# Memory matrix of the first attention: loaded as 32x32 squares and turned by VectorE instead of turned by TensorE

## The chip, the core and the metric

The kernel runs on one core of a Trainium2 chip. The metric is the device time of one execution in microseconds (us). TensorE (PE in the profile) multiplies matrices into PSUM; VectorE (DVE), ScalarE (ACT) and GpSimd (POOL) work on tiles in SBUF and PSUM; SyncE (SP) and GpSimd issue transfers, which sixteen DMA engines carry out. SP's transfers go through one queue, GpSimd's through another.

## The reference

Two transformer layers follow each other on an input of 2 x 512 rows of 512 values. Only the first attention is touched. It doesn't attend to other rows: each row is looked up in a memory `M` of eight 128x128 matrices.

```python
q = (hidden_states @ Wq.T + bq).reshape(b, s, H, D)     # H = 32, D = 128
sig_q = jax.nn.elu(q) + 1.0
q_sel = sig_q[:, :, ::G, :]                             # 8 of 32 heads, G = 4
num = jnp.einsum('bshd,hde->bshe', q_sel, M)
den = jnp.einsum('bshd,hd->bsh', q_sel, z)[..., None] + EPS
out_heads = jnp.repeat(num / den, G, axis=2)
output = out_heads.reshape(b, s, H * D) @ Wo.T
...
x = _layernorm(x + attention_0(x));  x = _layernorm(x + ffn_0(x))
x = _layernorm(x + attention_1(x));  x = _layernorm(x + ffn_1(x))
```

The feed-forward of layer 0 works with ternary weights and truncated 8-bit values, layer 1 has an ordinary softmax attention with one joint weight `Wqkv` (512 x 384) and an unquantized feed-forward. The result is the (2, 512, 512) tensor after the last layernorm, in 32-bit floats.

## The kernel before

Everything is on one core, with rows in tiles of 128 and features in blocks of 128. The kernel is written in program order; a scheduler orders the instructions of TensorE, VectorE, ScalarE and SP, and only GpSimd keeps the order of the program. `tc.issue_after` ties a step behind another. Tiles come from pools: a tile with the same tag as an older one gets its buffer and waits until that one is no longer read.

**Queries (0 to 62 us).** For each of 8 selected heads `h` and both batch rows `b`, the list `items` gives the order. `main_queries` issues 8 matmuls of 128x512 in split precision (a high part and a rest), ScalarE raises the result (`raise_main`, L364), and one item later `cross_queries` adds 4 more matmuls, ScalarE takes ReLU and exponential (L556, L557), and VectorE joins them to `q` (L560). `query_weights` splits the query weights, a part on ScalarE (L343) and two on VectorE (L344, L348).

**Folding the memory.** Since the four heads of a group share what is retrieved, the output weights of a group are summed first: SP loads half of them (`wos`, L429, 512 KB a head), GpSimd adds the other half with an accumulating transfer (L642), and `sum_weights` on VectorE adds the two halves of the tile (L574). `fold(h)` (L577) then multiplies the turned `M[h]` with this sum on TensorE (`pmw`, L579), and ScalarE writes it to `mw` (L581, L582). The last column of `mw` holds `z`, which GpSimd copies (L644); `mw` shares its buffer with `xt_raw`, the turned first input rows. For `fold`, `M` has to lie transposed: `turn_memory` (L562) turns its eight 128x128 blocks on TensorE against the identity into two PSUM banks, and ScalarE copies them back over `m` (L568).

The loop over `items` fixes what is done beside which item: `turn_memory` at `i == 4`, sums at `SUMS = [5, 6, 7, 8, 10, 11, 12, 13]`, folds at `FOLDS = [7, 8, 9, 10, 12, 13]` and two behind the loop.

**Loads.** SP issues, in this order: rows and query weights, `m` (512 KB, L422), wo0 to wo3, the gate/up weights gu0 to gu3 of layer 0 (L245, 512 KB each), `wqkv` (768 KB, L437), three biases and layer 1's output weight (L438 to L441), wo4 to wo7, and the other gate/up weights. wo4 to wo7 reuse the buffers of wo0 to wo3 and wait for their sums. GpSimd issues the eight accumulating transfers. SP's transfers use eight completion counters in turn, as do GpSimd's: a transfer waits until the one eight places before it on its queue's counters has landed.

**After that**, `read` (L584) multiplies queries with `mw` (L593), divides, adds and normalizes; then follow the feed-forward of layer 0, layer 1's attention and its feed-forward. In these stages rows are already turned in another way, which the change takes up: VectorE transposes each 32x32 square of a tile in place (`nc.vector.transpose`, L708), and `move_squares` (L301) then moves the squares to their turned places by transfers of 128-byte pieces, some issued by SP, some by GpSimd (L316).

Of the kernel before, what the change touches and what calls it, by code (L numbers as in the profile page):

```python
# [10 lines left out]
F32 = mybir.dt.float32  # L11
# [8 lines left out]
P = 128  # L20
B, S, HID = 2, 512, 512
NT = S // P
NK = HID // P
NH, G, D = 8, 4, 128
# [5 lines left out]
LAST = HID - 1  # L30
SQ = 32
# [8 lines left out]
def kernel(  # L40
# [19 lines left out]
    nc = tc.nc  # L60
# [3 lines left out]
    const = ctx.enter_context(tc.tile_pool(name="const", bufs=1))  # L64
# [7 lines left out]

    ident = const.tile([P, P], F32, tag="ident", name="ident")
    ones = const.tile([P, P], F32, tag="ones", name="ones")
    wqkv = const.tile([P, NK, 3 * D], F32, tag="wqkv", name="wqkv")
    bv = const.tile([P, D], F32, tag="bv", name="bv")
    wo1 = const.tile([D, HID], F32, tag="wo1", name="wo1")
    bo = const.tile([P, HID], F32, tag="bo", name="bo")
# [3 lines left out]
    def psum(name):  # L82
        return ps.tile([P, 512], F32, tag="mm", name=name)
# [13 lines left out]
    z = const.tile([D, NH], F32, tag="z", name="z")  # L97
# [141 lines left out]
    def up_weights(gu_in, name, chunks=range(len(CHUNKS))):  # L239
        gus = []  # L240
        for c in chunks:
            i, n = CHUNKS[c]
            gu = wffn.tile([P, 2, NK, n], F32, tag=f"gu{c}", name=f"gu{name}_{c}")
            at = 2 * HID * i
            nc.sync.dma_start(  # L245
                gu.rearrange("p a k i -> p (a k i)"),
                gu_in[at : at + 2 * HID * n].rearrange("(p f) -> p f", p=P),
            )
            gus.append(gu)
        return gus  # L250
# [75 lines left out]
    def pair_tile(name, dtype=F32):  # L326
        return wop.tile([P, 2, HID], dtype, tag="wo", name=name)
# [78 lines left out]
    with tc.tile_pool(name="a0w", bufs=1) as a0w, tc.tile_pool(name="a0", bufs=2) as a0:  # L406
# [12 lines left out]
            elif h == 2:  # L419
                load_x(1)  # L420
        m = a0w.tile([D, NH, D], F32, tag="m", name="m")
        nc.sync.dma_start(m, m_in)  # L422

        wos = []
        for h in range(NH):
            if h == 4:
                gus = up_weights(gu0_in, "0", range(EARLY))
            w = pair_tile(f"wo{h}")
            nc.sync.dma_start(w, wo0_in[h, :, : G // 2, :])  # L429
            wos.append(w)  # L430
# [3 lines left out]
        def late_loads():  # L434

            gus.extend(up_weights(gu0_in, "0", range(EARLY, len(CHUNKS))))
            nc.sync.dma_start(wqkv, wqkv_in.rearrange("(k p) f -> p k f", p=P))  # L437
            nc.sync.dma_start(bqk, bqk_in)  # L438
            nc.sync.dma_start(bv, bv_in.to_broadcast([P, D]))
            nc.sync.dma_start(wo1, wo1_in)  # L440
            nc.sync.dma_start(bo, bo_in.to_broadcast([P, HID]))  # L441


        hosts = [
# [22 lines left out]
        odd = single("t", 2, 2) + host(1)  # L467
# [94 lines left out]
        def turn_memory():  # L562

            for i in range(2):
                pt = psum(f"pt_m_{i}")
                for j in range(4):
                    nc.tensor.transpose(pt[:, ts(j, P)], m[:, 4 * i + j, :], ident)
                nc.scalar.copy(m[:, 4 * i : 4 * i + 4, :].rearrange("d h e -> d (h e)"), pt)  # L568

        def sum_weights(eng, h):  # L570

# [66 lines left out]
        qs = [{}, {}]  # L638
        pq = first_queries()
        mw = a0w.tile([D, NH, HID], F32, tag="mw", name="mw")  # L640
        for h in range(NH):
            nc.gpsimd.dma_start(wos[h], wo0_in[h, :, G // 2 :, :], accum_op=ALU.add)  # L642
            if h == 0:
                nc.gpsimd.tensor_copy(mw[:, :, LAST], z)  # L644
        query_weights(1, lows[1], lows[3])
        items = [(0, 1), (0, 2), (0, 3), (1, 1), (1, 2), (1, 3), (1, 0)]
        items += [(b, h) for h in range(NH // 2, NH) for b in range(B)]
# [4 lines left out]
        for i, (b, h) in enumerate(items):  # L652
# [11 lines left out]
                    later_rows(2 * i + k)  # L664
            if i + 2 < len(items) and items[i + 2][1] not in wq3:
                query_weights(items[i + 2][1], [*lows[3], *made] if i == 0 else ())
            if i == 4:
                turn_memory()
            if i in SUMS:
                with tc.issue_after(step.ins):  # L670
# [14 lines left out]
        fold(6)  # L685
        cross_queries(*held)
        fold(7)
        late_loads()
        order = [(b, t) for b in range(B) for t in range(NT)]
        checks += [(c, a) for c in range(EARLY, len(CHUNKS)) for a in range(2)]  # L690

# [923 lines left out]
```

## Time and profile before

| | us |
|---|---|
| median of 3 runs | 456.64 (455.45 to 456.96) |
| profiled execution | 456.56 |
| its span (first to last instruction) | 454.8 |
| TensorE matmul busy | 447.1 (98% of the span) |
| VectorE busy | 316.1 (69%) |
| ScalarE busy | 260.1 (57%) |
| GpSimd busy | 115.7 (25%) |

The profile shows one execution. A timeline line gives the start, the duration, the engine, the line of the program, the operation, output and input tiles, and how many instructions are merged; in brackets stands how long the engine was idle before and what ended this. Lines with SPq are issues of transfers: their duration is that of the issue, not of the transfer. Matmul ends are modelled, and neighbouring matmuls overlap, so starts are what to compare. A 32-bit matmul counts as two instructions. The strings of digits cut the span into 40 slices of 11.4 us; 9 means 90% busy or more. The chain of waits is followed back from the last instruction. The trace also records each DMA piece (packet) with its queue, size and duration, and the time at which each transfer landed.

### The profile page before, as it was taken

How to read it: one execution, taken by the hardware profiler on the slowest of the kernel's cores; microseconds unless marked ns; L12 is line 12 of the kernel's file. 1: busy time of each engine (PE TensorE's matmuls, PEld its weight loads, DVE VectorE, ACT ScalarE, POOL GpSimd, SP SyncE). 2: the span in 40 equal slices, each digit the busy share in tenths (PEclk: the TensorE clock that was granted, in tenths of full speed). 3: DMA queues.
4: the chain of work that ended last, by engine and by line, in shares of the span. 5: the costliest groups of instructions: out<-in, count | busy, mean ns of one | idle time of the engine just before them, and what ended most of it. 6: DMA issues, size and time to landing. Idle time of an engine off the chain costs nothing.

```text
span 454.8 us, 5802 instructions
## 1 busy us (share of the span) xinstructions
PE 447.1 (98%) x1905; PEld 334.6 (74%) x1905; DVE 316.1 (69%) x629; ACT 260.1 (57%) x494; POOL 115.7 (25%) x160
## 2 busy tenths in 40 slices
PE   8999999999999999999999999999999999999995
PEld 8887753344587888888766578888888888888884
DVE  4976657877886798847989899545534447777424
ACT  5788986467466975557745645454645446442311
POOL 0200305566650059201473237000000000012211
PEclk9999999999999999999999999999999999999998
DMA  8999990020028101131593502200000000000101
GB/s 280 386 270 317 180 333 8 0 38 12 1 47 235 42 2 48 48 94 38 176 350 69 94 1 43 51 0 1 0 0 1 0 1 1 0 25 24 46 26 68
DMA packets 33300, 38.18 MB, mean 84 GB/s; under 512 B 20784, under 2 KB 21680, under 8 KB 33264
## 3 DMA queue, kind: packets, MB, share of 16 engines
q1 hardware_dynamic: 30736, 31.05, 20.8%
q0 software_dynamic: 2240, 6.29, 7.5%
q8 instruction: 22, 0.36, 0.4%
q10 hardware_dynamic: 288, 0.36, 0.2%
q14 instruction: 14, 0.11, 0.1%
HBM read 32.45 MB, written 2.10 MB: 76 GB/s over the span
## 4 chain that ended last, share of the span: by engine, by line
PE 89%; ACT 5%; DMA 2%; issue 1%; DVE 1%; SPq 0%; POOL 0%; POOLq 0%
PE pu L1307 24%; PE pd L1307 12%; PE po L593 10%; PE pg_f L787 9%; PE pu_f L787 9%; PE pq L538 6%; PE pd_f L846 4%; PE pqk L1120 3%; ACT tu L374 2%; PE pu L1352 2%; PE pv L1137 2%; PE pot L1182 2%; PE po L1199 2%; PE psc L1076 2%; DMA wq<-in_wq 1%; DMA gu<-in_gu 1%
## 5 line engine op out<-in xcount | busy, mean ns | idle before, releaser
L593 PE MATMUL po<-mw,q 128*128 128x512 f32 x128 | 57.3, 599 | 0.3 <-DVE x L615 0.2
L146 POOL TENSOR_TENSOR rstd_f<-mv_f,ln_eps 128x1 f32<-128x1 f32 x15 | 6.7, 450 | 166.7 <-DVE mv_f L1475 128.7
L1307 PE MATMUL pu<-r,ugu 128*128 128x512 f32 x200 | 48.6, 389 | 0.0
L364 ACT ACTIVATE pu<-pu 128x512 f32<-128x512 f32 x42 | 24.2, 581 | 41.5 <-PE pu L1307 37.7
L593 PEld LDWEIGHTS po<-mw,q 128*128 128x128 f32 x128 | 22.6, 189 | 33.4 <-issue 17.2
L1307 PEld LDWEIGHTS pu<-r,ugu 128*128 128x128 f32 x200 | 37.5, 188 | 7.8
L170 ACT ACTIVATE ta_f<-y_f,below_half 128x512 int8<-128x512 f32 (+1 forms) x22 | 15.9, 722 | 27.4 <-DVE y_f L158 25.1
L615 DVE SCALAR_TENSOR_TENSOR x<-po,den,x 128x511 f32<-128x511 f32 x40 | 29.8, 745 | 1.9
L610 POOL TENSOR_TENSOR y<-y,y 128x511 f32<-128x511 f32 x16 | 21.3, 1333 | 23.9 <-DVE x L615 20.2
L1307 PE MATMUL pu<-r,it_early 128*128 128x512 f32 x104 | 24.9, 389 | 0.0
L1366 DVE TENSOR_TENSOR it_f<-ev,pu 128x512 f32<-128x512 f32 x20 | 13.7, 684 | 15.9 <-PE pu L1307 15.6
L1195 ACT ACTIVATE x<-x,off_f,rstd_f 128x512 f32<-128x512 f32 x7 | 5.7, 816 | 31.6 <-POOL off_f L1194 31.6
L813 DVE SCALAR_TENSOR_TENSOR it_f<-tb_f,ta_f 128x512 fp32r<-128x512 int16 (+1 forms) x22 | 15.6, 708 | 11.7 <-ACT tb_f L171 11.7
L1307 PE MATMUL pd<-ugu,r 128*128 128x512 f32 (+1 forms) x79 | 22.5, 362 | 0.0
L1307 PEld LDWEIGHTS pu<-r,it_early 128*128 128x128 f32 x104 | 19.5, 188 | 4.1
L787 PE MATMUL pg_f<-x,tu 128*128 128x512 f32 x88 | 22.1, 393 | 0.0
L787 PE MATMUL pu_f<-x,tu 128*128 128x512 f32 x88 | 21.7, 389 | 0.0
L376 POOL TENSOR_SCALAR td<-wd,inv_down 128x512 fp32r<-128x512 f32 x11 | 19.9, 1826 | 3.2 <-DVE inv_down L206 3.2
L846 PE MATMUL pd_f<-td,it_f 128*128 128x512 f32 x88 | 20.3, 389 | 0.0
L787 PEld LDWEIGHTS pg_f<-x,tu 128*128 128x128 f32 x88 | 16.4, 188 | 4.0 <-DVE x L615 0.4
L597 ACT ACTIVATE den<-po,den_eps 128x1 f32<-128x1 f32 x64 | 13.9, 272 | 9.3 <-PE po L593 9.1
L787 PEld LDWEIGHTS pu_f<-x,tu 128*128 128x128 f32 x88 | 16.5, 188 | 3.4
(390 smaller groups left out, 1111.2 us busy)
## 6 DMA issues: line engine op xcount, KB each, us to landing
gu<-in_gu SPq DMA_DIRECT2D x20, 512.0 KB, 7.1
wd<-in_wd SPq DMA_DIRECT2D x20, 256.0 KB, 4.9
wo<-in_wo SPq DMA_DIRECT2D x8, 512.0 KB, 8.8
wo<-in_wo POOLq DMA_DIRECT2D x8, 512.0 KB, 9.5
wq<-in_wq SPq DMA_DIRECT2D x8, 256.0 KB, 5.0
x<-in_x SPq DMA_DIRECT2D x7, 256.0 KB, 5.1
out<-x SPq DMA_DIRECT2D x7, 256.0 KB, 2.0
x<-in_bo POOLq DMA_DIRECT2D x4, 256.0 KB, 5.9
```

The lines of the kernel that those rows point to most:

```text
L170: nc.scalar.activation(a[:n], y, AF.Relu, bias=below_half[:n])
L364: return nc.scalar.activation(p, p, AF.Copy, scale=BIG + 1.0)
L376: eng.tensor_scalar(out, w, factor, None, ALU.mult)
L538: done = nc.tensor.matmul(p, w, x, start=(start and i == 0), stop=(i == len(todo) - 1), skip_group_check=not start,)
L593: nc.tensor.matmul(po, qs[b][h0 + j][:, ts(t, P)], mw[:, h0 + j, :], start=True, stop=True,)
L597: nc.scalar.activation(den[:, j : j + 1], po[:, LAST:], AF.Identity, bias=den_eps)
L610: nc.gpsimd.tensor_add(ys[0][:, :LAST], ys[0][:, :LAST], y[:, :LAST])
L615: steps.append(nc.vector.scalar_tensor_tensor(x[:, :LAST], four[j][:, :LAST], d, x[:, :LAST], ALU.mult, ALU.add))
L787: nc.tensor.matmul(pp[a], t[:, a, i % NK, :], x2[b][i], start=(i == 0), stop=(i == 2 * NK - 1),)
L813: nc.vector.scalar_tensor_tensor(it[:n], tb[:n], 128.0, ta[:n], ALU.min, ALU.subtract)
L846: nc.tensor.matmul(pd, inter[b][c][:, ts(t, P)], td[c].bitcast(F32R), start=(c == 0), stop=(c == last),)
L1307: done = nc.tensor.matmul(p, w, x, start=(start and i == 0), stop=(i == n - 1), skip_group_check=not start,)
```

## The change

`M` is no longer loaded as it lies and turned by TensorE. Sixteen transfers load its 32x32 squares to their turned places in a new tile `m_squares`: eight on SP, behind gu0 to gu3, and eight on GpSimd, ahead of the accumulating loads of `wo`. Each moves 8 heads x 32 rows of 128 bytes, 32 KB. VectorE then transposes each square in place with two 128x512 instructions, one for each half of the heads, into `m`. These two stand at `i == 6` instead of `i == 4`; in the built order the first lies on VectorE just ahead of the q and the sum of wo0, the second just behind that sum.

`m_squares` takes the buffer in which `wqkv` was, so `wqkv` is now a tile made in `late_loads`, with the same tag: its load waits for the second transpose and stands between wo4 and wo5 on SP. GpSimd's copy of `z` is moved ahead of everything else in that place.

```diff
-    wqkv = const.tile([P, NK, 3 * D], F32, tag="wqkv", name="wqkv")
+    m_squares = const.tile([P, 3, HID], F32, tag="wqkv", name="m_squares")
...
         m = a0w.tile([D, NH, D], F32, tag="m", name="m")
-        nc.sync.dma_start(m, m_in)
+        def load_memory(eng, odd):
+            dst = m_squares[:, :2].rearrange("p a (h i) -> p (a h) i", i=D)
+            for i in range(P // SQ):
+                for j in range(P // SQ):
+                    if (i + j) % 2 == odd:
+                        eng.dma_start(dst[ts(j, SQ), :, ts(i, SQ)], m_in[ts(i, SQ), :, ts(j, SQ)])
 
         wos = []
         for h in range(NH):
             if h == 4:
                 gus = up_weights(gu0_in, "0", range(EARLY))
+                load_memory(nc.sync, 0)
...
             gus.extend(up_weights(gu0_in, "0", range(EARLY, len(CHUNKS))))
+            wqkv = const.tile([P, NK, 3 * D], F32, tag="wqkv", name="wqkv")
             nc.sync.dma_start(wqkv, wqkv_in.rearrange("(k p) f -> p k f", p=P))
...
+            return wqkv
...
         def turn_memory():
             for i in range(2):
-                pt = psum(f"pt_m_{i}")
-                for j in range(4):
-                    nc.tensor.transpose(pt[:, ts(j, P)], m[:, 4 * i + j, :], ident)
-                nc.scalar.copy(m[:, 4 * i : 4 * i + 4, :].rearrange("d h e -> d (h e)"), pt)
+                turned = m[:, 4 * i : 4 * i + 4, :].rearrange("d h e -> d (h e)")
+                nc.vector.transpose(turned, m_squares[:, i])
...
         mw = a0w.tile([D, NH, HID], F32, tag="mw", name="mw")
+        nc.gpsimd.tensor_copy(mw[:, :, LAST], z)
+        load_memory(nc.gpsimd, 1)
         for h in range(NH):
             nc.gpsimd.dma_start(wos[h], wo0_in[h, :, G // 2 :, :], accum_op=ALU.add)
-            if h == 0:
-                nc.gpsimd.tensor_copy(mw[:, :, LAST], z)
...
-            if i == 4:
+            if i == 6:
                 turn_memory()
...
-        late_loads()
+        wqkv = late_loads()
```

## The prediction

> **What bounds the kernel now.** I read the page first (busy shares, chain), then the chain in order of time around the edited stage, then the timelines of the DMA queues and of VectorE there.
>
> ```profile
> PE   8999999999999999999999999999999999999995
> DMA  8999990020028101131593502200000000000101
> PE 89%; ACT 5%; DMA 2%; issue 1%; DVE 1%; SPq 0%; POOL 0%; POOLq 0%
> ```
>
> TensorE is busy in every fortieth of the span, and 89% of the chain is TensorE: what delays it anywhere is paid in full. The DMA engines are full only in the first six fortieths (to 68 us), and that is where the change works.
>
> ```profile
> 17.75 8.21 PE pq L538 x36
> 25.96 0.87 PE pt_m L567 x8
> 26.83 8.18 PE pq L538 x36
> 35.01 0.86 PE pmw L579 x2
> ```
>
> This is the chain in order of time (start, us). The eight transposes of the memory stand on it with 0.87 us. The first reader of the turned memory is `fold(0)` (pmw, first issued at 34.84 in TensorE's timeline).
>
> ```profile
> 10.47 0.43 SPq L422 DMA_DIRECT2D m<-in_m  x1
> 10.95 2.82 SPq L429 DMA_DIRECT2D wo<-in_wo  x4
> 14.14 2.90 SPq L245 DMA_DIRECT2D gu<-in_gu  x4
> 17.97 0.39 SPq L437 DMA_DIRECT2D wqkv<-in_wqkv  x1
> 19.99 0.34 SPq L438 DMA_DIRECT2D bqk<-in_bqk  x1
> 21.29 1.25 SPq L439 DMA_DIRECT2D bv<-in_bv  x1
> 22.58 3.43 SPq L440 DMA_DIRECT2D wo<-in_wo  x1
> 26.06 3.28 SPq L441 DMA_DIRECT2D bo<-in_bo  x1
> ```
>
> This is SP's queue. It has eight completion counters used in turn, so each transfer is issued only when the eighth before it has landed: wqkv, bqk, bv and wo1 are issued at 17.97, 19.99, 21.29 and 22.58, and the trace's landing records have wo0 to wo3 at 17.96, 19.98, 21.27 and 22.54. The last three issues take 1.25 to 3.43 us instead of 0.33 to 0.5: some 1250 pieces are outstanding then (counting 128 per 128-row load and 512 for wqkv), and the issue finishes as older ones land. The queue is backed up.
>
> ```profile
> L245 SPq DMA_DIRECT2D gu<-in_gu x4: 328/328/328, 14.1 to 16.7; - x4
> DMA to landing us min/median/max: 11.1/15.8/20.0
> ```
>
> The four gate/up loads before it land 11 to 20 us after issue, the last (gu3) at 16.7 + 20.0 = 36.7. In that time (22.6 to 37.8) they share the engines with GpSimd's four accumulating loads of `wo`; by the packet records the slowest engine moves one 4096-byte piece of each in turn (0.16 and 0.33 us), so the 32 pieces per engine of gu0 to gu3 need 14.0 us, 0.44 each.
>
> ```profile
> 29.60 0.69 DVE L348 TENSOR_TENSOR host_x<-host_t,host_t 128x512 fp32r<-128x512 f32 x1 [1.38 <-PE pq L538]
> 30.87 0.69 DVE L560 SCALAR_TENSOR_TENSOR q<-pq,r 128x512 f32<-128x512 f32 x1 [0.58 <-ACT pq L557]
> 31.48 0.68 DVE L574 TENSOR_TENSOR wos<-wo 128x512 f32<-128x512 f32 x1
> ```
>
> This is the place on VectorE where the changed kernel's built order puts the first memory transpose: after the first line, ahead of q and of `sum_weights(0)` (wos), which `fold(0)` reads. The second follows wos. So a late memory blocks not only itself but the sum.
>
> **The change part by part.**
>
> *Taken off.* TensorE: 8 transposes, 0.87 us of the chain. ScalarE: 2 copies of 0.60 us at 27.15, where it idles 0.46 us soon after (before L364 at 28.70): nothing. SP: the 512 KB load of `m`, ahead of wo0 in the queue; by the landing records it took from 15.43 to 16.70, 1.27 us.
>
> *VectorE.* Two 128x512 transposes at 0.71 us (the row of L708). By themselves they cost nothing: idle of 1.38, 0.58 and 0.83 us stands in 28.2 to 33.6, and the rows pushed back (L560, L344) feed TensorE only at 39 us or later. If that cover were gone they would cost 1.4 us.
>
> *GpSimd's queue.* The copy of z (0.55 us) goes first, at about 11.4, when the queries of item 0 release its buffer; then 8 square loads, some 0.7 us each (the row of L316 on POOL, 0.65 to 0.92), to about 18; then the accumulating loads, first issued at 18.27 before. So those start as before. Each square load is one piece of some 2 KB per engine if it is packed like the squares of L316 there (4 KB, about 0.3 us), so eight take some 8 x 0.15 = 1.2 us from the SP queue.
>
> *SP's queue, the step that decides.* The other 8 square loads stand behind gu3, in the place of wqkv. In the built order they wait for the counters of wo0 to wo3 and gu0 to gu3, one each. The eighth can be issued only when gu3 has landed.
> - gu3: if the 1.2 us of GpSimd's squares cancel the 1.27 us of `m`, it lands at 36.7 as before. If the squares cost nothing, the lead of 1.27 us is 8 pieces per engine at the contended 0.44, so 3.5 us: 33.2. Another upper bound is 37.8, when the accumulating loads end. I take 35.5, nearer to 36.7, because GpSimd's squares do have a duration.
> - From there to the last square: an SP square load lands 2.0 us after issue:
>
> ```profile
> xt_f<-squares SPq DMA_DIRECT2D x16, 32.0 KB, 1.9
> ```
>
>  Lower bound 0.1 + 2.0 = 2.1. But each has 256 pieces, twice bqk's, and the queue was full with less: the fifth should finish its issue only when gu3 is through, and sixth to eighth follow at 0.65 each (L316 at 91.9 to 103.2), so 1.35 + 2.0 = 3.35. I take 3.3, by the stretched issues of bv, wo1 and bo in this very place. All 16 loads write both halves, so the first transpose waits for the last: 38.8 (bounds 35.3 and 41.1).
> - Behind it on VectorE: transpose 0.71, q 0.6, wos 0.6 and a signal, 2.0 us in all. `fold(0)` starts at 40.8 (37.3 to 43.1) instead of 34.84: **+6.0 us** (+2.5 to +8.3). This contains the gain of the transposes, which is spent in the wait: TensorE comes to `fold(0)` at 33.97 and idles 6.8 us. After it VectorE's backlog runs at 0.6 each and stays ahead (the sums of `fold(1)` and `fold(2)` end near 43 and 45, needed near 44 and 48).
>
> *TensorE's clock.* It starts slow in this trace and drops again after the last matmul (near 449.1):
>
> ```profile
> 1.05 3.79 PE L113 MATMUL rise<-ones 128*128 128x128 f32 x16 [1.05 <-DVE below_half L108]
> 9.36 2.05 PE L509 MATMUL pq<-xt_raw,wq 128*128 128x128 f32 x16 [0.48 <-ACT xt_raw L484]
> 451.00:453.00 2.00, 0.00 (x0) 0.00 (x0) 0.39 (x1) 0.45 (x1) 0.22 (x1) 0.71 0.24 85
> 453.00:454.80 1.80, 0.00 (x0) 0.00 (x0) 0.00 (x0) 0.00 (x0) 0.00 (x0) 0.50 0.16 51
> ```
>
> Sixteen equal matmuls took 3.79 us at the start and 2.05 later; the seventh number of the windows is the granted clock, 0.50 some 4 us after the end. An idle of 6.8 us should cost one such slow start: 3.79 - 2.05 = **1.7 us** (0 if the clock holds, 1.9 if it lasts a little longer).
>
> *Later parts.* SP waits for the first sum with wo4, for the second transpose with wqkv, and wo5 to wo7 stand behind these: issued from about 40.5 instead of 32.19. The queue is empty then, wo4 lands within 3 us instead of 12.7, its accumulation takes 5.7 (45.48 to 51.19), so its sum is ready near 50, while its turn comes at 48.7 + 6: nothing. If that cover were gone, each us late is a us on `fold(4)`. wqkv is first read at 223.7: nothing. The gate/up loads from chunk 4 on wait for TensorE's last queries and shift with it, as does ScalarE's work on them at 64 to 69, which is on the chain.
>
> **Sum.** The profiled execution took 456.56 us (span 454.8 and 1.76 around it), 0.08 under the median of 456.64. 456.56 + 6.0 + 1.7 = **464.3 us**; by the bounds 459.1 to 466.8.
>
> One rule speaks further against the change. The row: sixteen SP loads of 128-byte pieces landed 1.9 us after issue (median) and the packet records show 13 ns a piece, 16 a load and engine. The Trainium skill's page "DMA: Bandwidth & Descriptors", section Specifications, asks for pieces of at least 512 bytes, since smaller ones are read, changed and written back. If that doubled the last four loads (4 x 0.21 us), the time would be about 465.1; by the row nothing is added. Both sources are in SBUF there, so the trace does not show such pieces read from memory in bulk.
>
> **The rivals.**
> - *The squares arrive in time (faster side).* If GpSimd's squares take turns with the SP queue by their 128-byte pieces, 16 x 8 pieces each behind a 4096-byte one (0.16), they last till after 30, the accumulating loads start late, and gu0 to gu3 run alone: 56 pieces after wo0 at 0.17 end near 27. The last square lands near 30 to 31, sum 0 near 33, and the gain is the whole 0.87 us: 455.7. It decides if the last square lands before 32.8 (34.84 less 2.0). For it: the order of the two queues on GpSimd changes. Against: L316's loads on POOL appear as single 4 KB pieces and landed within 3 us.
> - *The squares are late, the clock holds:* 462.6. Against: the clock's two rows.
> - *The square pieces alternate with what is left of the accumulating loads* (0.33 us a turn, some 8 turns): 2.6 us more, 466.9.
> - *No effect:* TensorE loses the transposes and waits as much elsewhere; the last square would have to land at 32.8 within 1.4 us, by chance: 456.6.
>
> **How the numbers follow.** Late squares 0.85 (within it 0.1 without the clock's loss, 0.1 with the alternation), in time 0.11, no effect 0.04. The late case's own range is 459.1 to 466.9. For 8 in 10 I widen it to 457.0 to 467.5, which leaves out the in-time case and a little at the top. About 0.3% (1.4 us) can be told from no change here; the in-time gain is 0.2%, so it mostly counts as same: faster 0.04, same 0.11, slower 0.85.
>
> **What would show it.** Right: VectorE idle for several us before the first memory transpose, released by a DMA of the squares, near 38.8; TensorE idle before the first pmw, released by VectorE; SP's later square issues stretched; granted clock 0.5 just after; everything later shifted alike. Wrong: the first transpose starts at 29 to 32 us, or gu3 lands near 27; or TensorE idles elsewhere, at the sums of wo4 to wo7 or the gate/up loads at 62 to 73 us.

## The result, and the profile after

The changed kernel took 465.88 us (median of 6 runs, 465.56 to 466.15), the kernel before 456.57 us (median of 6 runs beside it, 455.42 to 456.96). The ratio is 1.021, 95% interval 1.020 to 1.022: slower by 9.3 us. The forecast was 464.3 us with a range of 457.0 to 467.5. The profiled execution took 466.15 us, with a span of 464.2 (before 456.56 and 454.8).

The page first: TensorE in 40 slices of 11.6 us, the clock that it was granted, and the shares of the chain of waits.

```profile
PE   9994999999999999999999999999999999999994
PEclk9997999999999999999999999999999999999998
PE 85%; DMA 9%; DVE 1%; ACT 1%; issue 1%; POOL 0%; POOLq 0%; SPq 0%; DVEq 0%
```

One slice, the fourth (35 to 46 us), has lost half of TensorE's work and some of its clock; before it had neither. On the chain TensorE fell from 89% to 85%, and transfers rose from 2% to 9%. The chain in order of time (start, duration, what) says which transfers:

```profile
15.65 21.71 DMA m_squares<-in_m
41.30 2.05 PE pmw L587 x2
```

Before, this stretch was TensorE's queries, the eight transposes and more queries. Now 21.7 us of it are the squares' loads, and the first fold hangs on them. SP's queue (start, duration of the issues, line, output and input):

```profile
12.38 2.35 SPq L245 DMA_DIRECT2D gu<-in_gu  x4
15.65 19.72 SPq L429 DMA_DIRECT2D m_squares<-in_m  x8
37.38 0.34 SPq L447 DMA_DIRECT2D bqk<-in_bqk  x1
```

The issue of eight loads of 32 KB takes 19.7 us. By the landing records gu3 landed at 34.18; the single issues stand at 15.65, 17.21, 19.58, 21.84 (2.01 us long), 23.90 (6.78), 30.72 (3.35), 34.12 and 34.77, and all eight landed between 37.36 and 38.57. GpSimd's queue had no such trouble:

```profile
12.27 4.83 POOL L429 DMA_DIRECT2D m_squares<-in_m  x8
18.04 0.95 POOL L652 DMA_DIRECT2D wo<-in_wo  x1 [0.93 <-DMA m_squares<-in_m]
```

Its eight squares were issued in 4.8 us and landed from 17.74 to 22.54; in the packet records each is 16 pieces of 2048 bytes. SP's are 256 pieces of 128 bytes each. VectorE and TensorE at the place of the wait (in brackets the idle time before, and what ended it):

```profile
28.83 0.69 DVE L348 TENSOR_TENSOR host_x<-host_t,host_t 128x512 fp32r<-128x512 f32 x1 [0.49 <-PE pq L548]
39.27 0.71 DVE L576 STREAM_TRANSPOSE m<-m_squares 128x512 f32<-128x512 f32 x1 [9.76 <-DMA bqk<-in_bqk]
39.91 0.65 DVE L570 SCALAR_TENSOR_TENSOR q<-pq,r 128x512 f32<-128x512 f32 x1
40.49 0.67 DVE L582 TENSOR_TENSOR wos<-wo 128x512 f32<-128x512 f32 x1
```

```profile
33.16 1.07 PE L548 MATMUL pq<-host,host_y 128*128 128x512 f32 x4
41.30 2.05 PE L587 MATMUL pmw<-wos,m 128*128 128x512 f32 x2 [7.08 <-DVE wos L582]
78.47 3.70 PE L601 MATMUL po<-mw,q 128*128 128x512 f32 x8 [0.72 <-ACT y L614]
```

VectorE stood for 9.76 us in front of the first transpose. The name bqk in the bracket is inferred (it landed last before 39.27); what the transpose reads are the squares, landed at 38.57. The 0.70 us from there to 39.27 are VectorE's own waits: sixteen loads have signalled on sixteen semaphores, and eight instructions of its queue wait for two each at most, one after the other every 0.10 us (line L576 by engine and operation; duration min/median/max in ns, first and last start):

```profile
L576 DVEq EVENT_SEMAPHORE  x8: 21/50/50, 38.4 to 39.2; - x8
```

Behind the transpose come q and the sum of wo0, as they are built, and TensorE starts `fold(0)` at 41.30 instead of 34.84. Its two matmul instructions took 2.05 us together instead of 1.02 before, because the clock was at half. The windows (TensorE's clock is the seventh number after the stretch, then the share of the DMA engines, then GB/s):

```profile
36.00:42.00 6.00, 0.70 (x1) 0.50 (x2) 2.73 (x5) 1.24 (x2) 0.00 (x0) 0.64 0.53 112
42.00:44.00 2.00, 2.00 (x5) 1.01 (x3) 2.00 (x4) 0.58 (x2) 0.00 (x0) 0.50 0.96 227
44.00:46.00 2.00, 2.00 (x9) 1.64 (x8) 1.43 (x4) 1.06 (x3) 0.00 (x0) 0.86 0.96 292
```

The shift against before can be followed from start to start:

| start of | before | after | shift |
|---|---|---|---|
| `fold(0)` | 34.84 | 41.30 | 6.46 |
| pbc_up (L202) | 43.16 | 51.27 | 8.11 |
| first po | 62.61 | 70.72 | 8.11 |
| po after VectorE's x | 73.58 | 82.34 | 8.76 |
| end of span | 454.8 | 464.2 | 9.4 |

So 6.46 us are the wait, 1.65 the clock behind it, 0.65 one late gate/up load at 74 us, and the last 0.6 are spread over the rest.

### The profile page after: what moved, and what is told of

Same layout as the page of the kernel before. It is cut to its first block, busy times and chain, and to the rows that moved or that the text cites. A ratio compares the mean times of both kernels' runs of the same rounds, so it can differ in the third digit from the quotient of the medians.

```text
span 464.2 us, 5820 instructions
## 1 busy us (share of the span) xinstructions
PE 449.1 (97%) x1897; PEld 335.6 (72%) x1897; DVE 317.2 (68%) x631; ACT 259.1 (56%) x492; POOL 120.4 (26%) x168
## 4 chain that ended last, share of the span: by engine, by line
PE 85%; DMA 9%; DVE 1%; ACT 1%; issue 1%; POOL 0%; POOLq 0%; SPq 0%; DVEq 0%
PE pu L1315 23%; PE pd L1315 12%; PE po L601 10%; PE pg_f L795 9%; PE pu_f L795 9%; DMA m_squares<-in_m 5%; PE pq L548 4%; PE pd_f L854 4%; PE pqk L1128 3%; DMA x<-in_x 2%; PE pu L1360 2%; PE pv L1145 2%; PE pot L1190 1%; PE psc L1084 1%; PE po L1207 1%; PE pmw L587 1%
## 5 line engine op out<-in xcount | busy, mean ns | idle before, releaser
L364 ACT ACTIVATE pu<-pu 128x512 f32<-128x512 f32 x42 | 24.2, 581 | 41.6 <-PE pu L1315 37.7
L795 PE MATMUL pu_f<-x,tu 128*128 128x512 f32 x88 | 21.7, 389 | 0.0
```

What stands on the lines that cost most here:

```text
L364: return nc.scalar.activation(p, p, AF.Copy, scale=BIG + 1.0)
L795: nc.tensor.matmul(pp[a], t[:, a, i % NK, :], x2[b][i], start=(i == 0), stop=(i == 2 * NK - 1),)
```

## The experiments

The theory from the prediction was: the loads behind gu3 land too late, and TensorE pays the wait and a slow start of its clock. Two things are mixed in it, the place in SP's queue and the small pieces. All diffs are against the changed kernel unless they say otherwise; the time of the kernel before, on the same chip and beside the experiment, is given each time.

**1. The squares ahead of gu0 to gu3**

```diff
             if h == 4:
-                gus = up_weights(gu0_in, "0", range(EARLY))
                 load_memory(nc.sync, 0)
+                gus = up_weights(gu0_in, "0", range(EARLY))
```

> SP's eight square loads stand ahead of gu0 to gu3 instead of behind them; nothing else is edited (the built order then also puts both transposes earlier on VectorE). Theory (the place behind gu3 on SP's queue makes the memory late): the last square lands near 25 us instead of 38.6, the first transpose starts within 2 us of its turn, TensorE no longer idles 7 us before the first pmw, the clock stays at 1.00, and the time is the one before less the transposes, about 455.7 us, up to 457 if gu0 to gu3, now behind the squares, keep VectorE's maximum waiting. Rival (the 128-byte pieces are what is slow, wherever they stand): the squares still need some 15 us or hold up the loads behind them, and the time stays above 462.

Measured: 464.58 us against 455.57, ratio 1.020 (1.018 to 1.022). The theory missed by 8 us. The gu loads were no longer in front, and still the last square landed at 34.41, not near 25.

```profile
34.72 0.71 DVE L576 STREAM_TRANSPOSE m<-m_squares 128x512 f32<-128x512 f32 x1 [8.69 <-DMA gu<-in_gu]
39.50 0.68 DVE L582 TENSOR_TENSOR wos<-wo 128x512 f32<-128x512 f32 x1
```

```profile
37.26 1.56 PE L548 MATMUL pq<-host,host_y 128*128 128x512 f32 x4 [3.85 <-DVE q L570]
40.33 2.05 PE L587 MATMUL pmw<-wos,m 128*128 128x512 f32 x2 [1.51 <-DVE wos L582]
```

Part of this time is not the loads. The built order puts both transposes further forward on VectorE, so that more work stands behind them and ahead of the sum of wo0: from the start of the first transpose to `fold(0)` it took 5.61 us (34.72 to 40.33) instead of the changed kernel's 2.03. With the changed kernel's order `fold(0)` would have started near 36.8 (34.72 + 2.03, an estimate). That is still later than before (34.84), but by 1.9 us instead of 5.5. It was not run, so this run shows that the squares land late in this place too, and not how much of the 9 us that costs.

The landing records: SP's first three squares land at 23.58 to 23.93, as expected. Then GpSimd's accumulating loads of wo0 to wo3 start to move, and the others land at 27.51, 32.25, 34.03, 34.23 and 34.41; the accumulating loads land at 26.18, 28.77, 31.28 and 33.86. The transfers of the queues between 25.0 and 33.8 us (packets, MB, share of the sixteen engines; software_dynamic is GpSimd's queue):

```profile
q0 software_dynamic: 423, 1.52, 86.6%
q1 hardware_dynamic: 750, 0.59, 23.7%
```

GpSimd's queue moves 371 accumulating pieces of 4096 bytes, 327 ns each, and holds the engines for 87% of the stretch. SP's queue gets 577 of its 128-byte pieces through, one or two beside each of the big ones. A load of 256 such pieces has 16 on each engine, so it stands beside some 8 to 16 accumulating pieces of 0.33 us, 2.6 to 5.2 us a load. That is what the fourth and the fifth square show (3.58 and 4.74 us behind the one before); the last three follow when the last accumulating load has landed at 33.86. The place behind gu3 is thus not the only bad one: a place in which the squares meet the accumulating loads is bad too.

**2. One load in the old place**

```diff
         m = a0w.tile([D, NH, D], F32, tag="m", name="m")
+        nc.sync.dma_start(m_squares[:, :2].rearrange("p a (h i) -> p (a h) i", i=D), m_in)
...
-                load_memory(nc.sync, 0)
...
-        load_memory(nc.gpsimd, 1)
```

> The memory is loaded with one 512 KB transfer in the old place (ahead of wo0), straight into the buffer of the squares; the sixteen square loads are left out, so the blocks are turned only within their 32x32 squares and the output is not the reference's. The two VectorE transposes, the late wqkv and the early copy of z stay. Theory: all of these are free, time about 455.7 us (456.6 less 0.87). Rival (VectorE's added work, or wqkv between wo4 and wo5, costs): 457.5 us or more, with TensorE idle near 31 to 34 us or at the folds of wo4 to wo7.

Measured: 454.86 us against 455.57, ratio 0.998 (0.997 to 0.999). VectorE's transposes, the late `wqkv` and the early copy of `z` cost nothing; the eight transposes of TensorE are a gain of 0.7 us. That is the most that the idea brought in any run, and the 10 us between this and the changed kernel come from the way the memory is loaded (and from what the built order makes of it: here the transposes stand earlier on VectorE, at 25.73 and 26.92, and wait for nothing).

**3. Products on constants in the wait**

```diff
...
-            nc.tensor.matmul(p, m[:, h, :], wos[h], start=True, stop=True)
+            done = last_pass[-1]
+            for _ in range(24 if h == 0 else 0):
+                with tc.issue_after(done.ins):
+                    done = nc.tensor.matmul(p[:, :P], ones, ones, start=True, stop=True)
+            with tc.issue_after(done.ins) if h == 0 else ExitStack():
+                nc.tensor.matmul(p, m[:, h, :], wos[h], start=True, stop=True)
```

> The changed kernel, with 24 matmuls of 128x128 on constants put on TensorE just ahead of the first pmw, written into its bank and overwritten by it (some 6.2 us of work in the 7 us that TensorE waits). Theory (a part of the loss is the slow clock after the wait): the first pmw still starts near 41.3 us, but the granted clock stays near 1.00 after it and the time falls by 1.6 us against the changed kernel, to about 464.2. Rival (the clock costs nothing that the path feels, the loss after 41.3 us comes from VectorE's backlog): the time stays at 465.9, or rises.

Measured: 465.71 us against 455.57, ratio 1.023 (1.021 to 1.025): no gain. The squares came later in the profiled run (the last at 39.83), and the products ended too early:

```profile
33.84 5.52 PE L592 MATMUL pmw<-ones 128*128 128x128 f32 x48
42.47 1.12 PE L594 MATMUL pmw<-wos,m 128*128 128x512 f32 x2 [3.11 <-DVE wos L584]
```

```profile
42.00:44.00 2.00, 1.53 (x4) 0.96 (x5) 2.00 (x4) 1.49 (x4) 0.00 (x0) 0.92 0.63 215
44.00:46.00 2.00, 2.00 (x6) 1.56 (x5) 2.00 (x5) 1.16 (x2) 0.00 (x0) 0.50 0.77 199
```

3.1 us of idle time are left, the clock falls 1.2 us after work has begun again, and from `fold(0)` to pbc_up it takes 9.98 us, 1.66 more than before (8.32). So as a test of the clock it says nothing yet; run 4 repeats it with more products.

**4. More products on constants**

```diff
-            for _ in range(24 if h == 0 else 0):
+            for _ in range(38 if h == 0 else 0):
```

> The changed kernel with 38 instead of 24 filler products (128x128 on constants, 0.23 us each, to about 42.6) ahead of the first fold, so that TensorE does not idle there more than 1 us. Theory: the granted clock stays at 1.00 behind it and the 1.65 us between the fold and the first up-product are not paid: the stretch from the first fold to that product is 8.3 to 8.6 us instead of 9.98, time 464.0 to 464.9 (the filler itself may hold the fold back by up to 1 us). Rival (the slow clock is due to the fold's own work, not to the idle time): the stretch stays at 9.9 to 10, time 465.5 to 466.5.

Measured: 464.11 us against 455.7, ratio 1.018 (1.017 to 1.020).

```profile
33.70 8.64 PE L592 MATMUL pmw<-ones 128*128 128x128 f32 x76
42.54 1.12 PE L594 MATMUL pmw<-wos,m 128*128 128x512 f32 x2 [0.20 <-DVE wos L584]
```

```profile
42.00:44.00 2.00, 1.80 (x9) 1.04 (x8) 2.00 (x4) 1.49 (x4) 0.00 (x0) 1.00 0.49 175
```

`fold(0)` starts as late as in run 3, but the clock stays at 1.00 and pbc_up follows at 50.96, 8.42 us later instead of 9.98. The time is 1.6 us below that of run 3, the kernels before beside them being 0.1 us apart, and within the theory's range. The term for the clock is real and has the predicted size here. The wait itself is untouched.

**5. Folds four items later**

The loads as in the changed kernel; the transposes stand behind the q of item 8, and the folds 0 to 3 are taken from items 7 to 10 to items 9, 9, 10, 10.

```diff
-        FOLDS = [7, 8, 9, 10, 12, 13]
+        FOLDS = [9, 9, 10, 10, 12, 13]
...
-            if i == 6:
-                turn_memory()
+            if i == 8:
+                with tc.issue_after(step.ins):
+                    turn_memory()
+            for k in range(len(FOLDS)):
+                if FOLDS[k] == i:
+                    fold(k)
...
-            if i in FOLDS:
-                fold(FOLDS.index(i))
```

> The changed kernel with its loads as they are, but the transposes stand behind the q of item 8 on VectorE instead of ahead of sum 0, and folds 0 to 3 are made at items 9, 9, 10, 10 instead of 7, 8, 9, 10. Theory (only the order around the late memory costs, the folds have slack): the squares land late as before, near 38.6 us, the sums of wo0 to wo2 run in time, TensorE works on queries meanwhile, and the time is about 455.7 us, up to 457. Rival (late sums are not the point, SP's blocked queue is: wo4 to wo7 come too late behind the squares and wqkv): TensorE waits at the folds of wo4 to wo7 and the time stays above 459.

Measured: 462.0 us against 455.57, ratio 1.014 (1.012 to 1.015). The theory expected a full recovery and got about a third of it (9.3 us of loss became 6.4).

```profile
40.69 1.98 PE L587 MATMUL pmw<-wos,m 128*128 128x512 f32 x4 [1.73 <-DVE m L576]
55.52 2.05 PE L587 MATMUL pmw<-wos,m 128*128 128x512 f32 x2 [2.37 <-DVE wos L582]
```

The first wait shrinks from 7.08 to 1.73 us, but a second one appears at `fold(4)`: wo4 reuses the room of wo0, was issued at 40.36 behind the squares, and its accumulation landed at 54.75. In the changed kernel the wait at `fold(0)` covers these loads, since all of TensorE's later work shifts with it; with that wait mostly gone, they are what is late next.

**6. All squares on GpSimd's queue**

```diff
-                load_memory(nc.sync, 0)
...
+        load_memory(nc.gpsimd, 0)
         load_memory(nc.gpsimd, 1)
```

> All 16 squares are loaded by GpSimd's queue and none by SP's. Theory now: the cost is that SP's squares go out as 128-byte pieces that take turns, one for one, with the accumulating 4096-byte pieces of GpSimd's loads, while GpSimd's own squares are recorded as 2048-byte pieces and arrive in 5 to 6 us. Then the 16 squares are issued from 12.3 to about 22.5, the last lands at 27 to 28, the accumulating loads start about 5 us later (23 to 27 instead of 18 to 22) and end about 40 instead of 37.2; the first sum of weights needs the first of them, about 31 to 32, so fold(0) starts near 34.8 to 35.5 and the kernel needs 455.0 to 456.5, as before or a little less. Rival (small pieces cost the same on every queue, 256 x 32 rows in all): the last square lands at 38 or later, 463 to 466.

Measured: 457.23 us against 455.7, ratio 1.0035 (1.0022 to 1.0048): 7.7 us of the loss are gone, and 0.7 us more than was expected at most are left.

```profile
12.15 4.83 POOL L429 DMA_DIRECT2D m_squares<-in_m  x8
19.84 4.68 POOL L429 DMA_DIRECT2D m_squares<-in_m  x8 [2.86 <-DMA m_squares<-in_m]
25.38 3.63 POOL L652 DMA_DIRECT2D wo<-in_wo  x4 [0.86 <-DMA m_squares<-in_m]
```

The ninth waits for the first to land (eight counters in turn), the last lands at 29.78, the transposes run from 29.91 on, and `fold(0)` starts at 34.67. The accumulating loads, though, are issued from 25.38 and land at 33.81, 37.07, 39.98 and 43.16, the last 5.3 us later than before (37.83). VectorE's sums wait for each of them, and TensorE idles 0.60 us at `fold(0)`, 1.02 at pbc_up and 0.22 at `fold(4)`.

**7. SP's squares where the memory was loaded before**

Eight squares on each queue, but SP's ahead of wo0 to wo3.

```diff
+        load_memory(nc.sync, 0)
         wos = []
         for h in range(NH):
             if h == 4:
                 gus = up_weights(gu0_in, "0", range(EARLY))
-                load_memory(nc.sync, 0)
```

> SP's eight squares stand in the place where before loaded the whole memory: ahead of wo0 to wo3, so before the accumulating loads have started. Theory: with no accumulating load to take turns with, they land by about 23 to 25, wo0 to wo3 and the accumulating loads come about 5 us later, fold(0) starts at 35 to 36.5, time 455.7 to 458. Rival (SP's small pieces are slow wherever they stand, 3 to 4 us a load as in the run ahead of gu0): the last square lands after 34, the time is 463 to 466.

Measured: 459.41 us against 455.7, ratio 1.008 (1.006 to 1.009), between the two ranges. The squares themselves are quick here: with nothing accumulating, all sixteen land from 15.39 to 19.55, one every 0.28 us. But wo0 to wo3 are issued 4.1 to 5.0 us later and land at 21.47 to 26.05 (before 17.96 to 22.54), the accumulating loads at 31.22 to 41.82, and wo4 behind them is late:

```profile
53.60 0.69 DVE L582 TENSOR_TENSOR wos<-wo 128x512 f32<-128x512 f32 x1 [5.22 <-DMA wo<-in_wo]
```

```profile
54.35 1.12 PE L587 MATMUL pmw<-wos,m 128*128 128x512 f32 x2 [1.86 <-DVE wos L582]
```

```profile
55.00:55.40 0.40, 0.40 (x3) 0.16 (x2) 0.40 (x1) 0.00 (x0) 0.00 (x0) 0.98 1.19 236
55.40:55.80 0.40, 0.40 (x3) 0.31 (x2) 0.40 (x2) 0.29 (x2) 0.00 (x0) 0.50 0.91 174
58.60:59.00 0.40, 0.40 (x3) 0.30 (x2) 0.40 (x3) 0.11 (x1) 0.00 (x0) 0.76 1.08 215
```

1.86 us of idle time, and again the clock falls to 0.50, 1.0 us after work has begun again, until 58.8. Half of these 3.4 us is 1.7. The sum: `fold(0)` is 1.54 us earlier than before (33.30), TensorE then idles 1.12 us at pbc_up and 1.86 at `fold(4)`, and the clock takes 1.7, together 3.1 later; the first po is 3.3 later (65.90 against 62.61). So the theory's first half held (the small pieces pass quickly where nothing accumulates), and what stands behind them in the queue pays instead.

**8. One load in the new place**

The other corner: one load of 512 KB, no squares, behind gu3. VectorE's order is tied to that of the changed kernel, since the scheduler would have moved the transposes.

```diff
                 gus = up_weights(gu0_in, "0", range(EARLY))
-                load_memory(nc.sync, 0)
+                nc.sync.dma_start(m_squares[:, :2].rearrange("p a (h i) -> p (a h) i", i=D), m_in)
...
-                nc.vector.transpose(turned, m_squares[:, i])
+                with tc.issue_after((lows_done[-1], sums_done[0])[i].ins):
+                    nc.vector.transpose(turned, m_squares[:, i])
...
-        load_memory(nc.gpsimd, 1)
```

> The memory comes as one load of 512 KB (128 rows of 4096 bytes) on SP's queue, in the very place where the change has its eight squares, behind gu0 to gu3; GpSimd loads none of it, and VectorE, TensorE, ScalarE and GpSimd keep the changed kernel's order. The blocks aren't moved across partitions, so what is computed from the memory differs. With the run that had one load in the old place (454.86 us) and the one with the squares ahead of wo0 to wo3 (459.41) this separates place from size. Theory (the place behind gu3, whose 4096-byte pieces take turns with the accumulating loads, is most of the loss by itself): gu3 lands at 34 to 37, the one load 1.3 to 2 us behind it, the first transpose starts at 35.5 to 38.5, fold(0) 2 us later, 37.5 to 40.5 instead of 34.8, and with or without the slow clock's 1.65 us the time is 458 to 463. Rival (only the 128-byte pieces are late, a load of 4096-byte pieces in that place is hidden): fold(0) at 34.8 to 36, 455 to 457.

Measured: 462.58 us (460.62 to 463.85) against 455.75, ratio 1.013 (1.011 to 1.016), in the theory's range.

```profile
38.19 0.71 DVE L579 STREAM_TRANSPOSE m<-m_squares 128x512 f32<-128x512 f32 x1 [9.11 <-DMA m_squares<-in_m]
```

```profile
40.22 2.05 PE L590 MATMUL pmw<-wos,m 128*128 128x512 f32 x2 [6.43 <-DVE wos L585]
```

gu3 landed at 35.91 and the one load at 38.16, hardly sooner than the squares of the changed kernel (38.57). Here the transpose starts 0.03 us behind its landing, with one semaphore to wait for instead of sixteen. From `fold(0)` to pbc_up this execution (463.85 us, the slowest of the four) takes 10.91 us, 2.6 more than before: the clock came back only at 45.6. Runs 2, 7, 8 and the changed kernel make a table (ratio to before):

| | one load of 4096-byte rows | squares |
|---|---|---|
| ahead of wo0 to wo3 | 0.998 | 1.008 |
| behind gu3 | 1.013 | 1.021 |

The place costs 1.3 to 1.5%, the form 0.8 to 1.0%, and within the intervals the two add up. (In the left column GpSimd has no squares to load either. In the upper row the transposes stand earlier on VectorE, where they waited for nothing.) The place is the larger part: even one load of large pieces is too late for `fold(0)` behind gu3.

**9. The late weights alone**

The kernel before, with only the load of `wqkv` put off.

```diff
-    wqkv = const.tile([P, NK, 3 * D], F32, tag="wqkv", name="wqkv")
+    held_room = const.tile([P, 3, HID], F32, tag="wqkv", name="held_room")
...
+            wqkv = const.tile([P, NK, 3 * D], F32, tag="wqkv", name="wqkv")
             nc.sync.dma_start(wqkv, wqkv_in.rearrange("(k p) f -> p k f", p=P))
...
+            if i == 6:
+                with tc.issue_after(step.ins):
+                    nc.vector.memset(held_room[:, 0, 0:1], 0.0)
```

> The kernel before, with only the load of wqkv put off until after the queries' product of step 6 (it waits for a one-column write on VectorE to the same room). Theory: the late weights cost nothing, the time is that of before, within 0.3%. Rival: wqkv and the sums' second loads behind it push the late gate/up loads or wo4 back; then 457.5 to 462.

Measured: 455.67 us against 455.7, ratio 1.000 (0.999 to 1.001), with `wqkv` issued at 34.36 instead of 17.97. Putting `wqkv` off costs nothing.

**10. Four squares early on SP, twelve on GpSimd**

```diff
-                    if (i + j) % 2 == odd:
+                    if (i == j) != odd:
...
+        load_memory(nc.sync, 0)
         wos = []
...
-                load_memory(nc.sync, 0)
```

> Four squares on SP's queue in the place where before loaded the whole memory (ahead of wo0), twelve on GpSimd's: between the run with all sixteen on GpSimd (457.23, its accumulating loads 7 us late) and the one with eight of them ahead of wo0 on SP (459.41, wo0 to wo3 and so all accumulating loads 4 to 6 us late). wo0 to wo3 are issued 2.6 us later than before, the accumulating loads start at about 20.5 to 24 instead of 18 to 23. Theory (what is left of the loss in both runs is the delay of the accumulating loads, which the sums of weights wait for): the waits of the sums shrink to under 1 us in all, 455.3 to 456.8. Rival (the DMA engines are full up to 57 us, and sixteen loads of squares cost them the same wherever they stand): 457 to 459.

Measured: 456.67 us against 455.75, ratio 1.0025 (1.0013 to 1.0036). It is within the theory's range. It has the lowest median of the versions that load squares, though runs 6 and 11 are not told apart from it by their intervals, and it is still slower than before. `fold(0)` comes at 34.13, 0.71 earlier than before; the accumulating loads end at 40.32, and at `fold(4)` the lead is spent:

```profile
52.82 1.12 PE L587 MATMUL pmw<-wos,m 128*128 128x512 f32 x2 [0.67 <-DVE wos L582]
```

**11 and 12. Three gate/up loads out of the way**

Run 11 is run 10 with gu1 to gu3 loaded only behind the q of item 4; run 12 is the kernel before with the same move.

```diff
-                gus = up_weights(gu0_in, "0", range(EARLY))
+                gus = up_weights(gu0_in, "0", range(1))
...
+            if i == 4:
+                gus.extend(up_weights(gu0_in, "0", range(1, EARLY), step))
...
+            if behind is not None:
+                with tc.issue_after(behind.ins):
+                    nc.vector.memset(gu[:, 0, 0, 0:1], 0.0)
             nc.sync.dma_start(
```

> The version with four squares on SP's queue ahead of wo0 and twelve on GpSimd's (456.67 us against 455.75), and with gu1 to gu3 loaded only after the queries' product of step 4 on VectorE, at about 28 to 33 us behind wqkv and between wo4 and wo6, so that they no longer take turns with the accumulating loads of wo0 to wo3. Theory (what was left of the loss there is the accumulating loads, which ended at 40.3 instead of 37.8 and put back wo4 to wo7, so that the sum of wo4 came 0.67 us late for TensorE): the four accumulating loads end by 34 to 37, the sums' waits go, the 0.67 us go and the gain of 0.7 us of the run with one load in the old place is left: 454.8 to 455.6, ratio 0.998 to 1.000. Rival (gu2 and gu3 now stand between wo4 and wo6 and put those back as much, or come late for the comparisons on VectorE): 456 to 459.

> The kernel before with the same move of gu1 to gu3 alone (behind the queries' product of step 4, ahead of wo4 to wo7 on SP's queue). It had no wait of TensorE on the sums, so an earlier end of the accumulating loads of wo0 to wo3 gains nothing: 455.4 to 456.2, within 0.3% of before. Rival (wo4 to wo7, issued behind three more loads, come late for the sums): 457 to 460.

Measured: run 11 457.04 us against 455.75, ratio 1.0027 (1.0017 to 1.0038); run 12 455.55 us against 455.75, ratio 1.000 (0.999 to 1.001). In run 11 the rival was right, in run 12 the theory.

```profile
53.06 1.12 PE L590 MATMUL pmw<-wos,m 128*128 128x512 f32 x2 [1.28 <-DVE wos L585]
```

Without the gate/up loads beside them the four accumulating loads still land 3.0 to 3.4 us apart (29.86, 32.81, 36.17, 39.33), for 32 pieces on each engine at 0.33 us are 10.5 us by themselves. And the room that gu1 to gu3 left is taken again later: the accumulation of wo4 is issued 2.3 us sooner than before (43.16 against 45.48) but lands 1.1 us later (52.30 against 51.19), beside wo5 to wo7 and the moved gu2 and gu3.

No version that loads the squares was faster than the kernel before.

## Why the prediction was right, step by step

The sign, the mechanism and the size held: 464.3 us was predicted, 465.88 measured. By its own steps:

- *TensorE's and ScalarE's removed work, VectorE's transposes, the late `wqkv`.* Predicted as 0.87 us of gain lost in the wait, and nothing for the rest. Run 2 has the gain as 0.7 us, run 9 has the late weights at nothing. Right.
- *GpSimd's queue.* Predicted: about 0.7 us an issue, packed pieces, accumulating loads not later than before. Measured: 0.58 to 0.79 us, pieces of 2048 bytes, first accumulating load issued at 18.04 (before 18.27). Right. The pieces took 95 ns at the median, so the eight loads cost each engine 0.8 us and not the 1.2 of the sum.
- *gu3.* Predicted 35.5 (33.2 to 37.8), measured 34.18; in runs 3, 4 and 5, which have the same loads, 36.03, 36.67 and 37.32. The bounds hold the scatter.
- *From gu3 to the last square.* Predicted 3.3 us (2.1 to 3.35), measured 4.39, above the upper bound. This is a term that was mis-sized, and its bound was too tight. The issues were not the reason: the eighth came 0.59 us behind gu3 (1.35 in the sum), but it landed 3.80 us after its issue, not 2.0. Between 34.2 and 37.2 us the packet records show 1794 pieces of 128 bytes, 13 ns each, which is 1.5 us on each of sixteen engines, and 64 accumulating pieces of 327 ns, 1.3 us more; the last 67 small pieces follow until 37.87, and the last landing 0.70 us behind them. The 1.3 us are the third rival's mechanism (square pieces alternating with the accumulating loads), which had been kept out of the sum. Run 1 shows it in full.
- *First transpose and `fold(0)`.* The errors of the two steps above nearly cancel: the last square landed at 38.57, predicted 38.8. In the sum that is luck, since the two steps were sized apart. The runs show that they go together, though: in the changed kernel and runs 3, 4 and 5 the second step is 4.39, 3.80, 3.22 and 2.03 us, the shorter the later gu3 landed (34.18, 36.03, 36.67, 37.32), and the last square lands between 38.57 and 39.89 in all four. The transpose was put at once behind it and started 0.70 us later, at 39.27. This is a term that the sum did not have, the waits for sixteen semaphores; in runs 3 and 4 it is 0.70 and 0.71 us, in run 8, with one load, 0.03. From the transpose to `fold(0)` 2.0 were predicted and 2.03 measured, so `fold(0)` came at 41.30 instead of 40.8, and the wait is 6.46 instead of 6.0 us.
- *The clock.* 1.7 us predicted, 1.65 measured, and run 4 shows that this is due to the idle time. The upper bound of 1.9 holds for this run and not in general: run 8 paid 2.6. That the term came out so near is in part luck, since it depends on where in a step of the clock the work begins again (the last section has the steps): in the changed kernel 0.15 us after the start of one, in run 8 1.48 us after.
- *Later parts at nothing.* Here 1.3 us are missing, the largest part of what the sum lacks. 0.65 of it belongs to the third late gate/up load, issued at 68.27 and landed at 74.21 (before 60.16 and 65.22), for which ScalarE waited (second line). But in the profiled execution of the kernel before, ScalarE waited for the second of these loads too (first line):

```profile
63.99 0.72 ACT L374 ACTIVATE t<-gu,inv_up 128x512 fp32r<-128x512 f32 x1 [0.56 <-DMA gu<-in_gu]
74.23 1.34 ACT L374 ACTIVATE tu<-gu,inv_up 128x512 fp32r<-128x512 f32 x2 [1.21 <-DMA gu<-in_gu]
```

  That execution is no undisturbed base here: run 9 starts `fold(0)` and the first po within 0.03 us of it, does not wait in this place, and has the po after VectorE's x at 72.93 instead of 73.58. Against run 9 the changed kernel loses 1.3 us in this stage, against the profiled execution before 0.65. In runs 1, 3, 4 and 5 the same load landed 3.7 to 4.5 us after its issue and TensorE did not wait in that place. So the stall comes and goes between executions, with and without the change, and a late stage does not cause it in general; why the load took 5.94 us in this execution stays open, and so does the origin of the last 0.6 us. The sums of wo4 to wo7 were costed rightly at nothing, though their loads came later than predicted: wo4 landed 4.83 us after its issue (within 3 predicted) and its accumulation at 53.65 (near 50), while its sum had its turn at 56.78. This holds only while TensorE waits earlier: in run 5, where it doesn't, they cost 2.37 us.
- *The rule on pieces of at least 512 bytes* (the Trainium skill, "DMA: Bandwidth & Descriptors", section Specifications) would have doubled the last loads by the prediction's working. In the changed kernel between 34.2 and 37.2 us, and in run 7, the 128-byte pieces took 13 ns at the median, about as in the squares of L316 (13 in the prediction, 12 at the median of the records before). In run 1, beside the accumulating pieces, they took 27 ns, which is the double, but only 0.2 us more for a load and engine. What is dear there are the turns that they take with pieces of 327 ns.

Against the rivals: *in time* fell with the landing records (gu3 at 34.18, not near 27), *no effect* with the 7.08 us in front of `fold(0)`, *clock holds* with the windows. The theory after the result, that the place behind gu3 explained everything, fell with the landings in run 1; runs 2, 7 and 8 put place and form in its stead, and runs 6, 7, 10 and 11 show that the form also costs through the accumulating loads that it puts back.

## What to carry to other kernels

Where the DMA engines are full, what stands in front of a load and beside it in time decides when it lands: before an operand is moved in the order of issue, find the first reader's start and the landing time of what will then be ahead of it. An edit that takes 0.87 us from the bounding engine is lost at once if its operand comes through eight transfers of 2048 small pieces in all at the end of a backed-up queue. Splitting one load into sixteen also cost its reader the waits, 0.7 us here. And where a wait is taken off, look at once for the next late load, here wo4.

## What the runs showed of the hardware

- *The clock goes in steps of 3.41 us.* Taken from windows of 0.4 us (0.50 is slow, a value between gives the edge) and from the trace's record of the granted clock, the slow stretches were 37.7 to 44.6 us in the changed kernel, 37.9 to 44.7 in run 1 and 38.7 to 45.6 in run 8, each 6.8 us; 43.7 to 47.1 in run 3, 55.6 to 59.0 in run 5 and 55.4 to 58.8 in run 7, each 3.4 us.

```profile
37.40:37.80 0.40, 0.00 (x0) 0.00 (x0) 0.00 (x0) 0.00 (x0) 0.00 (x0) 0.91 0.09 13
44.20:44.60 0.40, 0.40 (x3) 0.31 (x2) 0.40 (x1) 0.08 (x1) 0.00 (x0) 0.56 0.91 218
```

  What is paid is half of the part in which TensorE had work again: 41.30 to 44.55 makes 1.6 (1.65 measured), 40.22 to 45.57 makes 2.7 (2.6 measured). The Trainium skill's page "TensorE: Matmul & The Clock Gate", section "What's actually happening", has a free-running window of 3413 ns, and the lengths agree with it. The edges do too: within each trace all of them lie whole multiples of 3.413 us apart, for example 7.01, 37.73, 44.55 and 460.98 in the changed kernel (9, 2 and 122 steps) and 4.18 and 55.38 in run 7 (15 steps).
- *About half a step without work is enough for the slow clock.* The skill's section names at least one idle window of some 3.4 us as the condition; the runs show less, so the measurement decides. If each trace is cut into steps from its first edge, the step before each of the six slow stretches had 1.86 to 3.41 us without TensorE work (1.86 in run 7: idle from 52.49 to 54.35 in the step 51.97 to 55.38). The largest idle time of a step at full clock with no slow stretch behind it was 1.73 us, up to the end of the last matmuls and in all runs (run 5: idle from 38.96 to 40.69 in the step 38.52 to 41.93); both idle times lie wholly inside one step, so the length is what separates these two. The bound thus lies between 1.73 and 1.86 us in these runs, with matmul ends that are modelled. A slow step with 1.48 or 1.52 us of idle time (runs 8 and 1) was followed by another slow one, as was the wholly idle one of the changed kernel, so these three stretches last two steps. No run was made to test the bound itself.
- *The same 32 KB square is 16 pieces of 2048 bytes from GpSimd's queue and 256 pieces of 128 bytes from SP's.* In the changed kernel GpSimd's landed 5.5 to 6.7 us after their issue and SP's, issued later, 3.8 to 21.7 us after.
- *Waiting for many transfers takes time of its own.* In the changed kernel, after the wait that the last landing ended, six more wait instructions stood ahead of the first transpose with nothing left to wait for, and still followed each other every 0.10 us.
- *Accumulating pieces take twice the time of plain ones*, 327 ns against 159 for 4096 bytes (run 1, 25.0 to 33.8 us), so the four accumulating loads of 512 KB hold all sixteen engines for 10.5 us.
